# Shared-expert down projections dealt over the token table of a routed expert layer, with the fillers, PSUM pools and first rows around the routing rearranged

## The chip, the cores and the metric

The kernel runs on one core of a Trainium2 chip. The metric is the device time of one execution in microseconds, given as the median of three runs. Engines are named as in the profile: PE is TensorE (PEld its weight loads), DVE is VectorE, ACT is ScalarE, POOL is GpSimd, SP issues most of the DMAs.

## What is computed

The input is x, 16 batches of 128 rows with 512 features, and a context of 16 times 128 rows with 128 features. The reference is one attention block and one mixture of experts, each added to x:

```python
x = x + _L0_xattn_ref(_layernorm(x, axis=-1), ctx_512, ctx_512)
x = x + _L0_ffn_ref(_layernorm(x, axis=-1), gate_weight, e_bias, w1, w2, w3, shared_w1, shared_w2, shared_w3)
...
    tidx, tw = _gate(x, gate_weight, e_bias)      # sigmoid, 4 of 8 groups, then 8 of 32 experts
    g = jnp.einsum('td,eid->tei', x, w1)
    u = jnp.einsum('td,eid->tei', x, w3)
    a = jax.nn.silu(g) * u
    routed = jnp.einsum('tei,edi,te->td', a, w2, comb)
    sh = jax.nn.silu(x @ shared_w1.T) * (x @ shared_w3.T) @ shared_w2.T
    out = routed + sh
```

There are 2048 tokens, each with 8 of 32 experts; an expert has 256 hidden features. The shared expert takes every token.

## The kernel before

A batch of 128 rows is one tile of 128 partitions. The order of the instructions on TensorE, VectorE, ScalarE and GpSimd is the order in which the program writes them (a manual schedule); each engine takes its own in that order, and a framework puts in the semaphores. The DMAs of SP stand in its queue in program order too. The work has four stages.

Attention (`attention_small`, to about 124 us) loops over 32 items, two halves of the heads for each of 16 batches. An item n issues its scores (line 430), the values of item n - 1 (446), the transposed queries of a later batch (`queries`, 417, with a copy on VectorE in 421), a few matmuls that only keep TensorE busy (`keep_warm`), and the output of item n - 2 (`added`). Lists named head and tail hang other steps onto an item, among them the layer norm's statistics (`layernorm_stats`), its inverse deviation (`first_rstd`, 11 small VectorE instructions) and the normalized rows (`rows_of`, 394). Before the loop stand the statistics of batches 0 and 1, then one `first_rstd` for both, then both rows, then the keys and values; `queries(0)` comes ahead of item 0, and `queries(b)` in item 2b - 2.

Routing (`route` in `experts`, about 133 to 165 us) is one long chain on VectorE: sigmoid scores, group sums, a comparison of groups (gt, eq, gm), masked scores (ms), a max8 and a match-replace for each of 16 batches, and the selection sel (1278). Then TensorE counts the tokens of each expert (1286, 1294) and ranks them (1316 to 1360).

To fill TensorE meanwhile, the up projections of the shared expert are a generator of single matmuls (`shared_up`, 253): 8 pieces of 8 matmuls of 512 columns, each piece a gate g (4 matmuls) and an up u (4), for 512 tokens and half of the hidden features. After g a silu on ScalarE is due (261), after u a product on VectorE (264, tile sa); both are put in lists and issued where the program says. The first piece uses two banks of a tile gu in the pool of the scores. The other 7 take banks from the pool ps_gu, two banks, opened when that pool has closed. `up_matmuls(n)` issues the next n of their 56 matmuls: 22 ahead of the routing's chain, 4 and 6 after the ranks, then 2 in each slot of the token table. In the chain, the product of the first piece stands behind gs, product0 (the second piece) behind the sum gt and ahead of gm, product1 (the third piece) behind the ninth max8.

The token table (165 to 214 us) lists which token stands at which place. Its loop has 16 slots, one per batch. A slot builds one-hot tiles hr (1076) and 6 of 8 hq (1085) on VectorE, the 2 other hq on GpSimd, ht (1083) on ScalarE, and adds 8 small matmuls to tok (1091). Each of hr, hq and ht has two buffers. Products and silus that wait are called between hq and the matmuls of a slot; a product waits one slot more in a list named held. In slots 4, 9 and 14 one shared down is issued (`shared_down`: four 512-column pieces on TensorE, 1420, two f32 matmuls), whose sum with x (1430) goes the way of the products, followed by a DMA of x to out. After the loop `finish_tokens` (1102, 1103) makes token, and the 13 other downs follow, each with its sum and its DMA.

The expert stage (236 us to the end) gathers 138 slices of 128 rows by indirect DMAs of GpSimd (1498), five ahead, transposes them (1512, copy 1514), runs the up matmuls (1534) and downs (1588), and scatters the weighted rows onto out by accumulating DMAs (1560). Weights of three experts are held; their first loads are issued from 163 us on.

At the end a flag is read. If an expert has more tokens than its capacity, or the attention's keys are too long, a general path behind a branch is run: the general attention, the experts again, and tiles of left-over tokens. With this input it isn't taken.

Of the kernel before, what the change touches and what calls it, by code (L numbers as in the profile page):

```python
# [43 lines left out]
def tile_xattn_moe(  # L44
# [24 lines left out]
    NTILES = (NT * P * TOPK + E * (P - 1)) // P  # L69
    LT = -(-NTILES // NW)  # L70
    NQT = LT * NW

# [199 lines left out]
    def attention_small():  # L272


        with ExitStack() as ph:
# [128 lines left out]
            for b in range(2):  # L404
                layernorm_stats(b, mv1)
            first_rstd(0, 2)
            for b in range(2):
                rows_of(b)
# [116 lines left out]

            for b, n in ((4, 1), (5, 1), (6, 2), (7, 2)):
                at_tail(n, layernorm_stats, b, mv1)
            for b in (2, 3):
                at_head(0, layernorm_stats, b, mv1)
            at_tail(0, first_rstd, 2, 2)  # L530
            at_tail(0, rows_of, 2)
# [41 lines left out]
            for n in range(N):  # L573
                for f, a in head.get(n, ()):
                    f(*a)

                scores(*items[n])
                if n > 0:
                    values(*items[n - 1])
                if n in parts:  # L580
                    gate_parts(parts[n])
                if n % 2 == 0 and n // 2 + 1 < B:
                    queries(n // 2 + 1)
                keep_warm(FILL.get(n, 0))
                if n in sums:
                    gate_sums(sums[n])
                if n > 1:
                    added(*items[n - 2])
                if n in turned:
                    gate_turn(turned[n], ps_tr)  # L590
                for f, a in tail.get(n, ()):
                    f(*a)
# [3 lines left out]
            ps_sc.tile([P, 2, G, P], F32, tag="sc", name="sc")  # L596
# [166 lines left out]
    def tile_work(ctx, token, owner, load_e):  # L763

        flat = out.rearrange("b s d -> (b s) d")
        wp = ctx.enter_context(tc.tile_pool(name="wp", bufs=1))

        wup = [wp.tile([P, 2, ND, I], F32, name=f"wup{r}") for r in range(NW)]  # L770
        wdn = [wp.tile([P, NI, D], F32, name=f"wdn{r}") for r in range(NW)]


        NG_BUF = 6
        xgs = [wp.tile([P, D + E], F32, name=f"xg{r}") for r in range(NG_BUF)]
        for t in xgs:
            nc.gpsimd.memset(t, 0.0)

        ps_gu = ctx.enter_context(tc.tile_pool(name="ps_gu", bufs=2, space=PSUM))
        ps_y = ctx.enter_context(tc.tile_pool(name="ps_y", bufs=2, space=PSUM))  # L780
        tp = ctx.enter_context(tc.tile_pool(name="tp", bufs=3))
        ps_a = ctx.enter_context(tc.tile_pool(name="ps_a", bufs=1, space=PSUM))
        ps_x = ctx.enter_context(tc.tile_pool(name="ps_x", bufs=2, space=PSUM))
        xg, xT, gus, al, aTs, last = {}, {}, {}, {}, {}, []

        def load_weights(q):
            r = q % NW
            with tc.issue_after(last[0]) if last else nullcontext():
                _, (e, new_e) = nc.values_load_multi_w_load_instructions(
                    load_e[0:1, :, q],  # L790
                    engines=[mybir.EngineType.SP],
                    min_val=0,
                    max_val=E - 1,
                    skip_runtime_bounds_check_because="experts' numbers and flags",
                    bass_reorder=False,
                )
            for dst, src in ((wup[r][:, 0], w1), (wup[r][:, 1], w3), (wdn[r], w2)):
                dma = nc.sync.dma_start(
                    dst,
                    src[bass.ds(e, 1)].rearrange("o p a b -> (o p) a b"),  # L800
                    **({} if q < NW else dict(cond=new_e, bounds_check="skip_entire_dma")),
                )
            last[:] = [dma.ins]

        def gather(q):
            t = xgs[q % NG_BUF]
            nc.gpsimd.indirect_dma_start(
                out=t,
                out_offset=None,
                in_=rows[:, :],  # L810
                in_offset=bass.IndirectOffsetOnAxis(ap=token[:, q : q + 1], axis=0),
                bounds_check=NT * P - 1,
                oob_is_err=False,
            )
            xg[q] = t

        def turn(q):
            tr = ps_x.tile([P, ND, P], F32, tag="trx", name="trx")
            for k in range(ND):
                nc.tensor.transpose(tr[:, k, :], xg[q][:, ts(k, P)], ident)  # L820
            t = tp.tile([P, ND, P], F32, tag="xT", name="xT")
            nc.scalar.copy(t, tr)
            xT[q] = t

        def up(q, ds):
            if 0 in ds:
                gus[q] = ps_gu.tile([P, 2, I], F32, tag="gu", name="gu")
            for d in ds:
                nc.tensor.matmul(
                    gus[q],  # L830
                    lhsT=xT[q][:, d, :],
                    rhs=wup[q % NW][:, :, d, :],
                    start=(d == 0),
                    stop=(d == ND - 1),
                )

        def gated(q):
            gu = gus.pop(q)
            del xT[q]
            sl = tp.tile([P, I], F32, tag="sl", name="sl")  # L840
            nc.scalar.activation(sl, gu[:, 0, :], AF.Silu)
            a = tp.tile([P, I], F32, tag="a", name="a")
            nc.vector.tensor_tensor(a, sl, gu[:, 1, :], ALU.mult)
            own = tp.tile([P, E], F32, tag="own", name="own")
            wt = tp.tile([P, 1], F32, tag="wt", name="wt")
            nc.vector.scalar_tensor_tensor(
                own,
                expert,
                owner[:, q : q + 1],
                xg.pop(q)[:, D:],  # L850
                ALU.is_equal,
                ALU.mult,
                accum_out=wt,
            )
            al[q] = a, wt

        def gated_turn(q):
            at = ps_a.tile([P, NI, P], F32, tag="at", name="at")
            for i in range(NI):
                nc.tensor.transpose(at[:, i, :], al[q][0][:, ts(i, P)], ident)  # L860
            aT = tp.tile([P, NI, P], F32, tag="aT", name="aT")
            nc.vector.tensor_copy(aT, at)
            aTs[q] = aT

        def down(q):
            aT, wt = aTs.pop(q), al.pop(q)[1]
            y = ps_y.tile([P, D], F32, tag="y", name="y")
            for i in range(NI):
                nc.tensor.matmul(
                    y,  # L870
                    lhsT=aT[:, i, :],
                    rhs=wdn[q % NW][:, i, :],
                    start=(i == 0),
                    stop=(i == NI - 1),
                )
            yw = tp.tile([P, D], F32, tag="yw", name="yw")
            nc.scalar.activation(yw, y, AF.Copy, scale=wt)
            nc.gpsimd.indirect_dma_start(
                out=flat,
                out_offset=bass.IndirectOffsetOnAxis(ap=token[:, q : q + 1], axis=0),  # L880
                in_=yw,
                in_offset=None,
                compute_op=ALU.add,
                bounds_check=NT * P - 1,
                oob_is_err=False,
            )

        def run(first, end):
            last.clear()
            for n in range(first - 4, end + 1):  # L890
                if first <= n + 4 < end:
                    gather(n + 4)
                if first <= n < end:
                    up(n, range(ND - 1))
                if first <= n - 1:
                    gated_turn(n - 1)
                if first <= n + 1 < end:
                    turn(n + 1)
                if first <= n < end:
                    up(n, [ND - 1])  # L900
                    gated(n)
                if first <= n - 1:
                    down(n - 1)
                if first <= n + 2 < end:
                    load_weights(n + 2)

        return run

    def rest():

        with ExitStack() as ctx:
            keep = ctx.enter_context(tc.tile_pool(name="keep", bufs=1))
            token = keep.tile([P, NQT], I32, name="token")
            owner = keep.tile([P, NQT], F32, name="owner")
            load_e = keep.tile([P, 2, NQT], I32, name="load_e")
            rounds = keep.tile([1, 1], I32, name="rounds")
# [816 lines left out]
```

## Time and profile before

| what | us |
|---|---|
| median of 3 runs | 1034.4 (1032.83 to 1034.75) |
| the profiled execution, its own time | 1034.52 |
| its span in the trace | 1032.7 |
| PE busy | 999.4 |
| POOL busy | 508.5 |
| ACT busy | 325.9 |
| DVE busy | 255.2 |
| VectorE's wait for a filler ahead of product0 | 3.58 |
| TensorE's waits for VectorE's one-hots, two | 0.96 and 2.27 |
| start of the first expert transpose | 236.13 |

Times within the trace count from the span's start. A row of the timeline has the start, the time to the end, the engine, the line, the operation, the tiles written and read, how many instructions were merged into it, and in brackets how long the engine was idle before it and what ended the idle time. An f32 matmul of the program appears as two in the trace. A row of the stage table has a stretch, its length, then the busy time of PE, PEld, DVE, ACT and POOL with their instruction counts, the granted TensorE clock (1.00 is full), the DMA share and GB/s.

### The profile page before, as it was taken

How to read it: one execution, taken by the hardware profiler on the slowest of the kernel's cores; microseconds unless marked ns; L12 is line 12 of the kernel's file. 1: busy time of each engine (PE TensorE's matmuls, PEld its weight loads, DVE VectorE, ACT ScalarE, POOL GpSimd, SP SyncE). 2: the span in 40 equal slices, each digit the busy share in tenths (PEclk: the TensorE clock that was granted, in tenths of full speed). 3: DMA queues.
4: the chain of work that ended last, by engine and by line, in shares of the span. 5: the costliest groups of instructions: out<-in, count | busy, mean ns of one | idle time of the engine just before them, and what ended most of it. 6: DMA issues, size and time to landing. Idle time of an engine off the chain costs nothing.

```text
span 1032.7 us, 12455 instructions
## 1 busy us (share of the span) xinstructions
PE 999.4 (97%) x4176; PEld 575.9 (56%) x4176; DVE 255.2 (25%) x902; ACT 325.9 (32%) x517; POOL 508.5 (49%) x658
## 2 busy tenths in 40 slices
PE   8999998999999999999999999999999999999993
PEld 5344444447666556676766666666644444444462
DVE  7887668951011000111111101101110010010100
ACT  5676612402222222232323232323222322322220
POOL 4588534732445445454545454545453445454342
PEclk9999999999999999999999999999999999999997
DMA  9011105053666757775757676767674766665541
GB/s 307 3 42 52 52 22 193 22 177 87 169 141 152 156 131 164 163 163 125 184 130 179 140 166 144 163 146 164 144 194 116 172 157 150 152 151 136 118 58 26
DMA packets 59865, 137.07 MB, mean 133 GB/s; under 512 B 12168, under 2 KB 16392, under 8 KB 59792
## 3 DMA queue, kind: packets, MB, share of 16 engines
q0 software_dynamic: 32032, 69.25, 35.5%
q1 hardware_dynamic: 27680, 66.81, 19.3%
q8 instruction: 35, 0.57, 0.2%
q14 instruction: 38, 0.31, 0.1%
q10 hardware_dynamic: 80, 0.13, 0.0%
HBM read 96.71 MB, written 46.73 MB: 139 GB/s over the span
## 4 chain that ended last, share of the span: by engine, by line
PE 64%; issue 5%; DMA 4%; POOL 3%; POOLq 0%; ACT 0%
PE gu L1534 40%; PE y L1588 19%; PE trx L1512 5%; DMA out_dram<-yw,token 4%; POOL out_dram L1560 2%; POOL xg L1498 1%; ACT xnT L1514 0%; POOLq L1560 0%; POOLq L1498 0%; POOLq L1659 0%
## 5 line engine op out<-in xcount | busy, mean ns | idle before, releaser
L1534 PE MATMUL gu<-xnT,wup 128*128 128x256 f32 (+8 forms) x1664 | 501.9, 450 | 2.4 <-ACT xnT L1514 2.4
L1534 PEld LDWEIGHTS gu<-xnT,wup 128*128 128x128 f32 x1664 | 313.1, 190 | 200.0 <-issue 134.1
L1560 POOL DMA_INDIRECT out_dram<-yw,token x150 | 235.7, 1571 | 368.0 <-ACT yw L1597 265.0
L1588 PE MATMUL y<-wdn,sa 128*128 128x512 f32 (+2 forms) x672 | 260.1, 594 | 0.0
L1545 DVE TENSOR_TENSOR sa<-sl,gu 128x256 f32<-128x256 f32 (+8 forms) x104 | 52.9, 508 | 699.0 <-PE gu L1534 681.8
L1498 POOL DMA_INDIRECT xg<-rows,token x138 | 145.3, 1053 | 61.1 <-issue 33.2
L1597 ACT ACTIVATE yw<-y,wt 128x512 f32<-128x512 f32 x138 | 94.8, 687 | 179.1 <-PE y L1588 153.9
L1588 PEld LDWEIGHTS y<-wdn,sa 128*128 128x128 f32 (+2 forms) x672 | 92.4, 171 | 72.7 <-issue 71.0
L1514 ACT COPY xnT<-trx 128x512 f32<-128x512 f32 (+3 forms) x150 | 81.3, 551 | 158.6 <-PE trx L1512 149.4
L1543 ACT ACTIVATE sl<-gu 128x256 f32<-128x256 f32 (+8 forms) x104 | 47.1, 453 | 247.7 <-PE gu L1534 243.0
L1512 PEld LDWEIGHTS trx<-ident,xg 128*128 128x128 f32 x552 | 69.0, 141 | 37.1 <-issue 26.2
L1512 PE MATMUL trx<-ident,xg 128*128 128x128 f32 x552 | 82.7, 273 | 0.0
L440 ACT ACTIVATE p<-sc 128x1024 f32<-128x1024 f32 x64 | 62.1, 1021 | 29.5 <-PE sc L430 29.5
L253 PE MATMUL gu<-xnT,sup 128*128 128x512 f32 x128 | 61.2, 617 | 3.9 <-ACT ssl L261 2.2
L1085 POOL TENSOR_SCALAR hq<-slice_q,sq 128x138 f16<-128x138 f16 x32 | 31.8, 1005 | 35.2 <-DVE sq L1386 23.0
L430 PE MATMUL sc<-qT,kz 32*128 32x512 f32 x256 | 41.8, 639 | 0.0
L253 PEld LDWEIGHTS gu<-xnT,sup 128*128 128x128 f32 x128 | 23.3, 195 | 28.4 <-issue 22.5
L446 PE MATMUL oT<-p,va 128*32 128x512 f32 x256 | 34.1, 605 | 1.1 <-DVE oTs L455 1.1
L475 POOL TENSOR_TENSOR x<-x,at 128x256 f32<-128x256 f32 x32 | 23.4, 734 | 22.8 <-DVE at L468 22.7
L1519 DVE SCALAR_TENSOR_TENSOR own<-expert,owner,xg 128x32 f32<-128x32 f32 x138 | 31.6, 246 | 0.0
L1420 PE MATMUL y<-sdn,sa 128*128 128x512 f32 x64 | 29.5, 615 | 0.0
L1083 ACT ACTIVATE ht<-hr,token 128x1024 f16<-128x1024 f16 x16 | 18.4, 1148 | 25.4 <-DVE hr L1076 22.6
(178 smaller groups left out, 468.2 us busy)
## 6 DMA issues: line engine op xcount, KB each, us to landing
wup<-in_w_dram SPq DMA_DIRECT2D x64, 512.0 KB
wdn<-in_w_dram SPq DMA_DIRECT2D x32, 512.0 KB
rows<-xn SPq DMA_DIRECT2D x16, 256.0 KB
out_dram<-x SPq DMA_DIRECT2D x16, 256.0 KB
x<-in_x_dram SPq DMA_DIRECT2D x15, 256.0 KB
out_dram<-yw,token POOLq DMA_INDIRECT x150
xg<-rows,token POOLq DMA_INDIRECT x138
cTs<-in_cT_dram SPq DMA_DIRECT2D x4, 256.0 KB
```

What stands on the lines that cost most here:

```text
L253: nc.tensor.matmul(acc, lhsT=sup[:, w, d, ts(i, P)], rhs=xnT[k][:, d, :], start=(d == 0), stop=(d == ND - 1),)
L430: nc.tensor.matmul(scs[j // 2][:, j % 2], lhsT=kzs[b // 4 % 2][rows, b % 4, i, :], rhs=qTs[b][rows], start=True, stop=True, tile_position= ...
L440: nc.scalar.activation(p, sc, AF.Exp, scale=1.0 / HD**0.5)
L1498: nc.gpsimd.indirect_dma_start(out=t, out_offset=None, in_=rows[:, :], in_offset=bass.IndirectOffsetOnAxis(ap=token[:, j : j + 1], axis=0) ...
L1512: nc.tensor.transpose(tr[:, d, :], t[:, ts(d, P)], ident)
L1514: nc.scalar.copy(xnT[n % NTB][:, :, col : col + b - a], tr[:, :, a:b])
L1534: nc.tensor.matmul(acc[:, 0:m], lhsT=wup[k % NW][:, w, d, ts(i, P)], rhs=xnT[n % NTB][:, d, 0:m], start=(d == 0), stop=(d == ND - 1),)
L1543: nc.scalar.activation(banks[2][:, 0:m], acc[:, 0:m], AF.Silu)
L1545: nc.vector.tensor_tensor(acts[n % NTB][:, i, 0:m], banks[2][:, 0:m], acc[:, 0:m], ALU.mult)
L1560: ins = nc.gpsimd.indirect_dma_start(out=flat, out_offset=bass.IndirectOffsetOnAxis(ap=token2[:, k - 1 : k] if a else token[0:b, j : j + 1 ...
L1588: nc.tensor.matmul(y[c0:c1, :], lhsT=acts[n % NTB][:, i, col : col + c1 - c0], rhs=wdn[pieces[n][0] % NW][:, i, :], start=(i == 0), stop=( ...
L1597: nc.scalar.activation(yws[j], y, AF.Copy, scale=wt[:, j : j + 1])
```

## The change

It has four parts.

1. Ahead of the attention's loop stand the statistics, `first_rstd` and rows of batch 0 alone, then the statistics of batch 1. One `first_rstd` for batches 1 to 3 stands at the tail of item 0 with the row of batch 1; the row of batch 2 goes to the tail of item 1. The queries of batch 1 go from item 0 to item 1, ahead of `queries(2)` in item 2.
2. Around the routing: 20 fillers instead of 22 ahead of the chain, 4 and 9 instead of 4 and 6 after the ranks; product0 behind ms instead of ahead of gm. An unused tile that turned the pool of the scores by one is dropped, and the pools ps_gu and ps_y are opened in the other order. In the built program the first piece stays in banks 0 and 1 and the later pieces move from banks 0 and 1 to 2 and 3, the downs the other way.
3. The shared downs: one in each odd slot from 1 to 11, two in each of slots 12 to 14, one in slot 15, and 3 after the table. In slots 13 to 15 the products and sums no longer wait the further slot.
4. The general path behind the branch is another one: it reads the rows and logits back, and runs every expert over every token, weighted by zero where the main path did the work. The number of left-over tiles and its loops are gone.

The main path's instructions are the same in number but for one wait, and the order on ScalarE, GpSimd and SP is the same; on TensorE and VectorE the order differs as said.

```diff
             fixed_values(0, nc.vector)
-            for b in range(2):
-                layernorm_stats(b, mv1)
-            first_rstd(0, 2)
-            for b in range(2):
-                rows_of(b)
+            layernorm_stats(0, mv1)
+            first_rstd(0, 1)
+            rows_of(0)
+            layernorm_stats(1, mv1)
...
+            for b in (2, 3):
+                at_head(0, layernorm_stats, b, mv1)
+            at_tail(0, first_rstd, 1, 3)
+            at_tail(0, rows_of, 1)
+            at_tail(1, rows_of, 2)
             for b, n in ((4, 1), (5, 1), (6, 2), (7, 2)):
                 at_tail(n, layernorm_stats, b, mv1)
-            for b in (2, 3):
-                at_head(0, layernorm_stats, b, mv1)
-            at_tail(0, first_rstd, 2, 2)
-            at_tail(0, rows_of, 2)
...
-                if n % 2 == 0 and n // 2 + 1 < B:
+                if (n == 1 or n % 2 == 0 and n > 0) and n // 2 + 1 < B:
                     queries(n // 2 + 1)
...
-            ps_sc.tile([P, 2, G, P], F32, tag="sc", name="sc")
             gu = ps_sc.tile([P, 2, G, P], F32, tag="sc", name="gu")
...
+        ps_y = ctx.enter_context(tc.tile_pool(name="ps_y", bufs=2, space=PSUM))
         ps_gu = ctx.enter_context(tc.tile_pool(name="ps_gu", bufs=2, space=PSUM))
-        ps_y = ctx.enter_context(tc.tile_pool(name="ps_y", bufs=2, space=PSUM))
...
-            up_matmuls(22)
+            up_matmuls(20)
...
             nc.vector.tensor_tensor(gt, gt, eq, ALU.add)
-            product0()
             gm = new([P, NQ], "gm")
...
             nc.vector.tensor_scalar(ms, ms, 0.0, None, ALU.add)
+            product0()
...
-            up_matmuls(6)
+            up_matmuls(9)
...
             held = list(products)
+            if b > NT - NTB:
+                meanwhile += held
+                held.clear()
             later.clear()
...
             up_matmuls(2)
-            if b % 5 == 4:
+
+            for _ in range(b % 2 if b < NT - NTB else 2 if b < NT - 1 else 1):
                 shared_down(next(downs))
...
     with tc.If(left > 0, preferred_fallthrough_block=False):
-        flag = nc.values_load(
...
-        with tc.If(flag > 0):
-            attention_general()
-            experts(pieces, ExitStack(), [], [])
         rest()
```

## The prediction

> **What bounds the kernel now.** I read the page first, then TensorE's waits, then the timelines of TensorE and VectorE around the routing, then a table by stage. The page:
>
> ```profile
> PE 999.4 (97%) x4176; PEld 575.9 (56%) x4176; DVE 255.2 (25%) x902; ACT 325.9 (32%) x517; POOL 508.5 (49%) x658
> PE 64%; issue 5%; DMA 4%; POOL 3%; POOLq 0%; ACT 0%
> ```
>
> TensorE is busy for 97% and carries the chain that ended last. The view of TensorE's waits, cut to the time after 240 us, has one row of 1.7 us (on the copy xnT of line 1514): the expert stage has next to no slack, so it starts later or earlier as a block, with its tail of scatter DMAs. The change touches nothing in it. So I ask only when its first transpose (236.13 us) starts. TensorE before it:
>
> ```profile
> 137.65 19.15 PE L253 MATMUL gu<-xnT,sup 128*128 128x512 f32 x44 [1.70 <-DVE sa L264]
> 157.23 0.55 PE L1286 MATMUL count<-ones,sel 128*32 128x1 f16 x16 [0.43 <-DVE sel L1278]
> ...
> 160.68 5.42 PE L253 MATMUL gu<-xnT,sup 128*128 128x512 f32 x12
> 168.32 5.40 PE L253 MATMUL gu<-xnT,sup 128*128 128x512 f32 x8 [2.23 <-ACT ssl L261]
> 173.56 0.66 PE L1091 MATMUL tok<-hq,ht 128*128 128x138 f16 x8
> 174.05 1.93 PE L253 MATMUL gu<-xnT,sup 128*128 128x512 f32 x4
> ...
> 206.40 0.67 PE L1091 MATMUL tok<-hq,ht 128*128 128x138 f16 x8 [0.96 <-DVE hq L1085]
> 209.33 0.67 PE L1091 MATMUL tok<-hq,ht 128*128 128x138 f16 x8 [2.27 <-DVE hq L1085]
> 209.84 2.96 PE L1420 MATMUL y<-sdn,sa 128*128 128x512 f32 x4
> 212.60 1.12 PE L1091 MATMUL tok<-hq,ht 128*128 128x138 f16 x8
> 213.52 22.77 PE L1420 MATMUL y<-sdn,sa 128*128 128x512 f32 x52
> 236.13 1.04 PE L1512 MATMUL trx<-ident,xg 128*128 128x128 f32 x8
> ```
>
> A row counts each f32 matmul of the program twice. From 204.8 to 213.5 TensorE waits for VectorE's one-hot tiles (hq), while 13 shared downs stand idle until 213.52. The gaps are followed by slow rows: 8 pieces took 5.40 us, against 19.15/44 = 0.435 us a piece elsewhere. The stage table, whose third number from the end is the granted clock, says why:
>
> ```profile
> 168.35:173.56 5.21, 5.21 (x9) 2.10 (x10) 2.08 (x8) 1.15 (x1) 1.69 (x2) 0.67 1.00 403
> 204.80:213.52 8.72, 5.49 (x38) 3.28 (x36) 6.56 (x22) 3.44 (x3) 4.25 (x5) 0.83 0.01 2
> ```
>
> VectorE in the routing:
>
> ```profile
> 144.89 0.69 DVE L264 TENSOR_TENSOR sa<-ssl,gu 128x512 f32<-128x512 f32 x1 [3.58 <-PE gu L253]
> 151.76 0.69 DVE L264 TENSOR_TENSOR sa<-ssl,gu 128x512 f32<-128x512 f32 x1
> 156.49 0.69 DVE L1278 TENSOR_TENSOR sel<-rp,ms 128x512 f16<-128x512 f32 x1
> 213.76 0.30 DVE L1102 TENSOR_SCALAR empty<-tok 128x138 f32<-128x138 f32 x1 [2.40 <-PE tok L1091]
> ```
>
> **What the skill says.** The Trainium skill, "TensorE: Matmul & The Clock Gate", section "What's actually happening": the clock falls to half after a mostly idle window of 3413 ns; windows run free. The trace agrees: 0.50 granted from about 169.6 to 173 us and from about 210.4 to 213.8, after windows with 2.2 and 2.3 us of idle; the 1.70 us of idle before 137.65 left it at 1.00. "DMA: Bandwidth & Descriptors", section "Anatomy of one DMA — SWDGE (gpsimd) path": about 2.0 us plus bytes/436e3. A gather of 128 rows of 2176 bytes is then an estimated 2.6 us behind its issue of 1.0 to 1.3. Agrees: the gather issued at 214.71 had its 0.28 MB moved by 218.5 in the DMA view.
>
> **Part 1, rows of batch 0 alone.** The chain from statistics 0 to row 0 no longer waits for statistics 1: it begins at 4.82 instead of 6.25, -1.43 us. Behind row 0 on VectorE now stands statistics 1 (0.85), which fits under the four transposes (the copy qT starts 8.70, was 10.12). Scores 0, exp 0, scores 1 and values 0 all come 1.43 earlier (values 0 at 13.75, was 15.17). But the transposes of batch 1 now follow values 0: copy oTs at 14.93, copy qT at 15.53, and scores 0.80 behind it: item 2 at 16.33, where it was 16.16. It then no longer waits for ScalarE (0.27 saved), so values 1 starts at 17.40 against 17.51. Row 1 waits for x of batches 1 to 3 (landed before 9.2, since the later-queued cn landed at 9.18); it is ready at 14.15, needed at 14.74. Sum **-0.1 us**; bounds -1.4 (all kept) and +0.7 (row 1 late).
>
> **Part 2, product moved and 20 for 22 fillers.** Moving product0 behind ms lets VectorE run on instead of idling 3.58 us, so it reaches product1 at about 149.0. But product1 needs the 16th filler matmul: 137.65 + 32 x 0.4288 is 151.4, and it already started at 151.76 as TensorE ended. So it waits there 2.7 us and sel stays at 156.49: nothing gained. The banks swap places, yet in the built order the first filler of the second piece still waits for the first product (the 1.70 us above), so that stays too; bounds -1.7 and 0, taken 0. With two fillers fewer TensorE stops at 155.1 and idles 2.2 us before the counts.
>
> After the counts (160.68 in both) 4 + 9 fillers stand in place of 4 + 6. The 8 before the next wait take 8 x 0.858 + 0.27, to 167.8; ScalarE's silu then gives 168.6 (it gave 168.32). The idle there falls from 2.23 to 0.8, so this window should not halve the clock. Net **+0.3 us** at the start of that matmul, and the same 28 fillers are left in both.
>
> **Part 3, the spread downs.** Work from there: 28 fillers (4 at 0.87, 2 lone ones at 0.86, 11 pairs at 1.77 as between 174.05 and 175.82) 24.7; 16 table groups at 0.49, 7.85; 16 downs at 22.61/13 = 1.74, 27.8; sum 60.4. Before took 236.13 - 168.32 = 67.8, so 7.4 was lost: half clock 1.97 and about 1.6, waits 0.38 + 0.96 + 2.27. If these go, the expert stage starts at 168.6 + 60.4 = 229.0: **-7.1 us**, part 2's 0.3 within it.
>
> Does VectorE keep up? A slot costs it 1.14 (hr) + 1.15 (hq) = 2.29, against TensorE's 2.26 without a down, 4.0 with one, 3.97 with two and no fillers. It gets 10 more adds of 0.6 ahead of the table, 6.0, but its 3.39 us wait at 173.82 shrinks by 1.5. In the built order an add stands behind the one-hots of a later slot than its down, so TensorE has a table group and new downs while VectorE adds. In slots 13 to 15 VectorE needs 0.3 + 1.2 + 2.3 = 3.8 per slot from the end of a pair of downs, TensorE 0.49 + 3.48 = 3.97: 0.2 to slack. GpSimd's two hq take about 2.1 of the 4 us between table groups. The SP queue has the same 16 writes of out, now from slot 3 on, behind the loads of expert weights that ended by 174.
>
> The cover: 13 downs (22 us) hid the gathers; now 4 do, 7.0 us. Table end 222.0, token and gather issue 0.95 + 0.3, landing 3.6 more: about 227, the second 1.6 later at 228.5; needed at 229.0 and 229.5. Cost 0, up to +2 (plus 1.7 of half clock) if landings spread as between 220 and 227.7, where seven gathers took 1.9 us each beside the writes.
>
> **Part 4, the dense path** stands behind a branch that is not taken: no instruction of it runs. Taken 0, bounds -0.3 and +0.3.
>
> Sum: -0.1 - 7.1 = -7.2 us. The profiled execution took 1034.52 (span 1032.7), 0.12 above the median 1034.4: **1027.3**.
>
> **Rivals.** (a) The idle before the counts halves the clock: its window holds 1.3 us of idle, then 32 tiny matmuls; half clock over the rank matmuls and first fillers costs about 1.5: 1028.8. For: two such windows above; against: 1.70 us of idle did not. (b) Gathers uncovered: +2 to +3.5: 1030.3. (c) The slots fall partly into step, losing 0.45 each of 16: 1034.4, no change. (d) Slower: VectorE's adds wait in its queue for y ahead of the next one-hots, and TensorE waits for those. Full lockstep is 0.49 + 3.48 + 0.3 + 0.6 + 2.3 = 7.2 a slot against 4.0, over 9 slots +29; half of it ends at 1034.5 - 7.2 + 14 = 1041. It decides against the change from 7.2/9 = 0.8 us a slot on. Against it speaks the slot of lead. (e) The wait on the banks or on product1 does not bind as I read it: 1.5 to 3 better, 1025.
>
> **Chances.** Forecast 0.58 (own range 1025.5 to 1029), a 0.17, b 0.08, c 0.05, d 0.05, e 0.07. About 0.2% (2 us) is what a measurement can tell from no change: faster 0.90, same 0.05, slower 0.05. The range 1024.0 to 1031.5 takes in forecast, a, b and e.
>
> **What would show it.** VectorE idle about 2.7 us ahead of the product between the max8 steps; TensorE idle 2.2 before count and under 1 before the u of the fifth piece; clock 1.00 at 168 to 214; no wait for hq over 0.5; first expert transpose near 229, no wait for xg over 1. Wrong if rows tok wait for hq in each slot, or trx waits for a gather.

## The result, and the profile after

| | before | after |
|---|---|---|
| median | 1033.62 us (4 runs) | 1024.76 us (4 runs, 1022.55 to 1025.06) |
| ratio, 95% interval | | 0.9909 [0.9891, 0.9927], so -9.4 us [-11.3, -7.5] |
| profiled execution, its own time | 1034.52 | 1022.55 |
| its span | 1032.7 | 1020.8 |
| first expert transpose | 236.13 | 230.21 |
| from there to the start of the last scatter's issue | 781.59 | 782.24 |
| from there to the end of the span | 15.02 | 8.33 |

The change is faster: 9.4 us are gained where 7.2 were forecast, and the median is 2.5 us under the forecast of 1027.3. The last three rows already say that the forecast's own account is wrong: the expert stage starts 5.9 us earlier and not 7.1, it gets 0.65 us longer, and 6.7 us are won at the very end, where the forecast put nothing (-5.92 + 0.65 - 6.69 = -11.96, the difference of the two spans).

The page of the kernel after, the two lines that answer to those of before:

```profile
PE 996.8 (98%) x4176; PEld 574.3 (56%) x4176; DVE 254.3 (25%) x902; ACT 326.2 (32%) x517; POOL 513.1 (50%) x658
PE 77%; POOL 9%; issue 7%; DVE 4%; DMA 2%; ACT 1%; POOLq 0%; DVEq 0%; ACTq 0%
```

TensorE's work is the same. Its timeline around the routing (start, time to the end, in brackets the idle time ahead):

```profile
137.39 17.43 PE L250 MATMUL gu<-xnT,sup 128*128 128x512 f32 x40 [1.72 <-DVE sa L261]
156.96 0.55 PE L1135 MATMUL count<-ones,sel 128*32 128x1 f16 x16 [2.14 <-DVE sel L1127]
...
159.93 1.75 PE L1167 MATMUL rank<-sel,ones 128*128 128x352 f16 x11
161.99 7.13 PE L250 MATMUL gu<-xnT,sup 128*128 128x512 f32 x16
169.87 4.56 PE L250 MATMUL gu<-xnT,sup 128*128 128x512 f32 x10 [0.75 <-ACT ssl L258]
...
223.29 7.08 PE L1269 MATMUL y<-sdn,sa 128*128 128x512 f32 x16
230.21 0.60 PE L1365 MATMUL trx<-ident,xg 128*128 128x128 f32 x4
231.29 0.66 PE L1365 MATMUL trx<-ident,xg 128*128 128x128 f32 x4 [0.49 <-DMA xg<-rows,token]
```

The waits for one-hot tiles are gone: from 174 to 230 TensorE has no wait. The bank wait (1.72) and the 2.14 us ahead of the counts are there as forecast. The fillers behind the ranks start at 161.99, not at 160.7. The table by stage shows why (its third number from the end is the granted clock):

```profile
157.92:161.33 3.41, 3.41 (x17) 1.54 (x14) 2.02 (x10) 0.00 (x0) 0.00 (x0) 0.50 0.00 0
161.33:164.70 3.37, 3.37 (x17) 1.74 (x16) 2.49 (x13) 0.59 (x1) 0.00 (x0) 1.00 0.00 0
```

Half clock lay over the rank matmuls: rival (a). On VectorE the third piece's product (product1) waits as forecast, and sel starts at 156.22:

```profile
151.50 0.69 DVE L261 TENSOR_TENSOR sa<-ssl,gu 128x512 f32<-128x512 f32 x1 [2.67 <-PE gu L250]
```

Last, the end of GpSimd's stream: the issue of the last scatter in the timeline, then rows of the view by source line, for the branch and for the kernel's end (number of instructions, shortest, median and longest in ns, start of the first and last). Before:

```profile
1017.71 1.57 POOL L1560 DMA_INDIRECT out_dram<-yw,token  x1 [0.30 <-issue]
L1665 POOLq EVENT_SEMAPHORE  x6: 17/30/43, 1018.0 to 1021.6; - x6
L1665 POOLq COMPARE_BRANCH  x2: 41/42/43, 1017.9 to 1023.4; - x2
L1665 POOLq INC_SWDGE_SEM  x1: 1612/1612/1612, 1021.7 to 1021.7; - x1
L1729 POOLq DRAIN  x3: 46/107/5982, 1025.9 to 1032.5; - x3
```

After:

```profile
1012.45 1.57 POOL L1413 DMA_INDIRECT out_dram<-yw,token  x1 [0.30 <-issue]
L1518 POOLq COMPARE_BRANCH  x2: 41/42/43, 1012.6 to 1012.9; - x2
L1518 POOLq EVENT_SEMAPHORE  x2: 17/17/17, 1012.7 to 1012.8; - x2
L1573 POOLq DRAIN  x3: 46/113/6562, 1013.4 to 1020.5; - x3
```

In the kernel before GpSimd enters the short side of the branch, the one that skips the general path, at 1017.9, 0.2 us behind the start of its last scatter. It waits there for its eight DMA lanes (the eight semaphores in which its DMAs report in turn) until 1021.7, runs an instruction of 1.6 us that counts the lanes' semaphores up (INC_SWDGE_SEM), and jumps to the kernel's end at 1023.4. There its long Drain instruction starts at 1025.9, and the other engines wait for that Drain at the last barrier. In the kernel after it jumps at 1012.9 and the Drain starts at 1013.4, beside the scatter that is still on its way. The built program says where the waits come from: on the short side, each engine brings every semaphore to the value that the general path would have left. The old general path issues gathers and scatters from GpSimd, on all eight lanes; the dense path issues none.

### The profile page after: what moved, and what is told of

Read it like the earlier page. It is cut to its first block, busy times and chain, and to the rows that moved or that the text cites. A ratio compares the mean times of both kernels' runs of the same rounds, so it can differ in the third digit from the quotient of the medians.

```text
span 1020.8 us, 12451 instructions
## 1 busy us (share of the span) xinstructions
PE 996.8 (98%) x4176; PEld 574.3 (56%) x4176; DVE 254.3 (25%) x902; ACT 326.2 (32%) x517; POOL 513.1 (50%) x658
## 4 chain that ended last, share of the span: by engine, by line
PE 77%; POOL 9%; issue 7%; DVE 4%; DMA 2%; ACT 1%; POOLq 0%; DVEq 0%; ACTq 0%
PE gu L1387 44%; PE y L1441 21%; PE trx L1365 6%; PE gu L250 3%; POOL hq L935 2%; POOL out_dram L1413 2%; POOL xn L214 2%; DMA out_dram<-yw,token 1%; POOL x L471 1%; PE sc L426 1%; DVE st L88 1%; POOL kz L347 1%; PE oT L442 1%; DMA xg<-rows,token 0%; DVE oTs L451 0%
## 5 line engine op out<-in xcount | busy, mean ns | idle before, releaser
L935 POOL TENSOR_SCALAR hq<-slice_q,sq 128x138 f16<-128x138 f16 x32 | 35.2, 1113 | 40.8 <-DVE sq L1235 24.6
```

The lines of the kernel that those rows point to most:

```text
L935: engine(k).tensor_scalar(hq[:, k, :], tile_q, sq[:, b, k : k + 1], None, ALU.is_equal)
```

## The experiments

Theory T, formed from these two traces: of the gain, 6.7 us at the end are part 4's. The rival is the prediction on record: part 4 is worth 0, and part 3's 7.1 us carry the change. Times are compared as ratios with runs of the kernel before taken beside each experiment on the same chip (three sets of runs, medians 1032.9, 1032.8 and 1034.5).

**Part 4 alone.** The kernel before with the dense path in `rest`, and the old `tile_work` and the two calls behind the branch gone.

```diff
     with tc.If(left > 0, preferred_fallthrough_block=False):
-        flag = nc.values_load(
...
-        with tc.If(flag > 0):
-            attention_general()
-            experts(pieces, ExitStack(), [], [])
         rest()
```

> The kernel before with part 4 alone (the dense path behind the branch; nothing else). As the prediction has it, part 4 costs nothing: 1033.6, and the expert stage as well as the end as before. Theory T, formed from the two traces: in the kernel before GpSimd waits, on the side of the branch that is taken, until the last scatters have landed, and only then begins the Drain of about 6 us that closes the kernel; the new path behind the branch issues no DMA from GpSimd, so that this wait is not there and the Drain runs beside the last scatter. T expects the stretch from the start of the last scatter's issue to the end of the span to fall from 15.0 to about 8.4 us, the first expert transpose to stay at 236.1, and 1027.0 in all.

Measured 1027.75 us, ratio 0.9949 [0.9937, 0.9962], -5.3 us. In its profile the last stretch is 8.33 us, as in the kernel after. The end, in the view by source line:

```profile
L1516 POOLq COMPARE_BRANCH  x2: 41/42/43, 1016.2 to 1016.4; - x2
L1571 POOLq DRAIN  x3: 46/113/6563, 1016.9 to 1024.0; - x3
```

The transposes start at 234.39, not 236.1, for a reason outside this part: this execution had one stretch of half clock, the profiled one of before two. Part 4 is not free of effect; the prediction's zero falls. The trace's 6.69 us lie just outside the interval of the times, 3.9 to 6.5. With five runs, half clock that falls in some executions and not in others can make that difference, but this is not shown.

**Part 3 alone.**

```diff
             held = list(products)
+            if b > NT - NTB:
+                meanwhile += held
+                held.clear()
...
-            if b % 5 == 4:
+            for _ in range(b % 2 if b < NT - NTB else 2 if b < NT - 1 else 1):
                 shared_down(next(downs))
```

> The kernel before with part 3 alone (the spread downs, 22 and 6 fillers as before). As the prediction has it: first expert transpose at 228.7 (236.1 less 7.4), no wait for one-hots over 0.5 us, clock 1.00 from 168 to 214, and 1033.6 - 7.4 = 1026.2. Rival: the gathers are not covered, the transposes wait for them, and half clock stays somewhere: transpose at 230 to 232, 1028 to 1030. Either way the end stays as before: 15 us from the start of the last scatter's issue to the end of the span.

Measured 1029.16 us, ratio 0.9963 [0.9948, 0.9977], -3.8 us: half of what was forecast for it. No wait for one-hots is left. But the profile shows half clock behind TensorE's 2.21 us of idle time ahead of the matmul that needs the silu, the transposes of the second slice wait 0.77 us for its gather, and the first start at 230.34. The rival of this run holds. TensorE's timeline:

```profile
168.31 5.40 PE L253 MATMUL gu<-xnT,sup 128*128 128x512 f32 x8 [2.21 <-ACT ssl L261]
231.70 0.66 PE L1516 MATMUL trx<-ident,xg 128*128 128x128 f32 x4 [0.77 <-DMA xg<-rows,token]
```

**Eight gathers behind the branch.** The kernel after; `idx` is an index tile, and none of these gathers is run.

```diff
             comb = keep.tile([P, NT, E], F32, name="comb")
...
+            got = keep.tile([P, D + E], F32, name="got")
+            for _ in range(8):
+                nc.gpsimd.indirect_dma_start(
+                    out=got,
...
```

> The kernel after, with eight gathers issued by GpSimd added in the path behind the branch, which is not run with this input; all instructions that are run ahead of the branch are the same. If part 4 costs nothing (the prediction), 1024.8 as the kernel after. Theory T: the waits of GpSimd for its eight DMA lanes come back on the side of the branch that is run, the Drain starts only after them, and the stretch from the start of the last scatter's issue to the end is 15 us again: 1024.8 + 6.6 = 1031.4, with the first expert transpose at 230.2 as in the kernel after.

Measured 1028.64 us, ratio to before 0.9951 [0.9937, 0.9965] where the kernel after had 0.9909; the last stretch is 12.73 us instead of 8.33. What is built ahead of the branch is the same, instruction for instruction. Instructions that never run cost 4.4 us, through the waits that they put on the short side. The rows of the branch and the end in the view of source lines, of this run:

```profile
L1530 POOLq COMPARE_BRANCH  x2: 41/42/43, 1011.8 to 1017.1; - x2
L1530 POOLq INC_SWDGE_SEM  x1: 1612/1612/1612, 1015.4 to 1015.4; - x1
L1585 POOLq DRAIN  x3: 46/107/5982, 1017.5 to 1024.1; - x3
```

The theory's 15 us were too many by 2.3: the Drain follows the jump 0.4 us later here and 2.5 us later in the kernel before. So a second cost remained, which the run with memsets takes alone.

**22, 4 and 7 fillers.** The kernel after with TensorE's idle time ahead of the counts filled again.

```diff
-            up_matmuls(20)
+            up_matmuls(22)
...
-            up_matmuls(9)
+            up_matmuls(7)
```

> The kernel after with 22 fillers ahead of the chain and 4 and 7 behind the ranks (20, 4 and 9 in the kernel after): the two fillers go back into TensorE's idle time ahead of the counts. Theory H (the half clock over the rank matmuls comes from that idle time, rival a of the prediction): idle ahead of the counts 0.4 instead of 2.1 us, clock 1.00 from 157 to 162, fillers behind the ranks start at 160.4 instead of 162.0, and the expert stage 1.3 to 1.6 us earlier: 1023.3. Rival: the idle time moves to the next wait (the u of the fifth piece waits for its silu, as in the kernel before with 2.2 us), halves the clock there, and nothing is gained: 1024.8.

Measured 1022.96 us, ratio to before 0.9894 [0.9879, 0.9908]; the kernel after had 0.9909 and, below, 0.9900. The time can't tell them apart. In the profile theory H is right at its place (idle 0.43 us ahead of the counts, fillers at 160.41, full clock) and so is its rival one step on: the wait for the silu is 2.21 us again and half clock follows it. TensorE's timeline of this run:

```profile
156.96 0.55 PE L1135 MATMUL count<-ones,sel 128*32 128x1 f16 x16 [0.43 <-DVE sel L1127]
160.41 5.42 PE L250 MATMUL gu<-xnT,sup 128*128 128x512 f32 x12
168.03 6.25 PE L250 MATMUL gu<-xnT,sup 128*128 128x512 f32 x10 [2.21 <-ACT ssl L258]
```

**Memsets behind the branch.** The kernel after, with no DMA of GpSimd behind the branch but 190 more instructions of its own there.

```diff
+            pad = keep.tile([P, 1], F32, name="pad")
+            for _ in range(190):
+                nc.gpsimd.memset(pad, 0.0)
```

> The kernel after with 190 small memsets for GpSimd added in the path behind the branch, which is not run: as many GpSimd instructions behind the branch as in the kernel before, but no DMA of GpSimd. In the kernel before 2.5 us pass between the end of GpSimd's branch and its Drain, in the kernel after 0.5. Theory J: that jump is longer where more of GpSimd's own instructions lie behind the branch; 2.5 us here too, the stretch from the last scatter's issue to the end 10.4 instead of 8.3, 1026.9. Rival: the jump goes with the waits for the DMA lanes, not with the length; 8.3 us and 1024.8 as the kernel after.

Measured 1026.75 us, ratio to before 0.9937 [0.9923, 0.9951] where the kernel after had 0.9909, and the last stretch is 10.79 us, 2.46 more. The Drain starts 3.5 us behind the jump, with no wait between them, as the same view of this run shows:

```profile
L1521 POOLq COMPARE_BRANCH  x2: 41/42/43, 1011.4 to 1011.6; - x2
L1576 POOLq DRAIN  x3: 46/107/5988, 1015.1 to 1021.7; - x3
```

Theory J's rival falls: the jump gets longer with no DMA behind the branch. J itself holds only in part, for the jump takes 3.5 us and not 2.5, and it does not grow with the number of instructions. In the built programs GpSimd jumps over some 90 of its instructions in the kernel after, 110 with the gathers, 280 with the memsets and 2100 in the kernel before; the jumps take 0.46, 0.46, 3.49 and 2.55 us. That is a step between 110 and 280 instructions, not a slope.

A step fits what the Trainium skill, "Runtime: NRT & Kernel Launch", section "Instruction fetch mechanics", says of a branch that is taken: if the target lies outside the fetched window, its page must be loaded before the engine goes on. The DMA view agrees where it is clear of other engines: cut to the jump of the kernel before (1023.36 to 1025.89) it has a single packet, of an instruction queue; cut to that of the gathers' run (1017.08 to 1017.53) it has none. Why the load takes 2.5 us in one kernel and 3.5 in another is not known.

So part 4's 6.7 us are 5.2 of waiting and counting up (5.64 and 0.46 us from the start of the last issue to the jump), 2.1 of a longer jump, less 0.6 because the Drain takes 6.56 beside a scatter and 5.98 otherwise.

**Part 2 alone.** The kernel before with 20, 4 and 9 fillers, product0 behind ms and the pools in the other order.

```diff
-            up_matmuls(22)
+            up_matmuls(20)
...
-            product0()
             gm = new([P, NQ], "gm")
...
             nc.vector.tensor_scalar(ms, ms, 0.0, None, ALU.add)
+            product0()
...
-            up_matmuls(6)
+            up_matmuls(9)
```

> The kernel before with part 2 alone (20 fillers ahead of the chain, 4 and 9 behind the ranks, product0 behind ms, the pools in the other order). The prediction: sel starts where it did (156.5), TensorE idles 2.2 us ahead of the counts at full clock behind it, the idle time ahead of the next silu falls from 2.2 to 0.8 us with no half clock behind it: 0.3 us lost and 2.0 of half clock won against the profiled execution of before. Rival a: the half clock moves from the silu's gap to the counts; the rank matmuls end 1.3 us later, nothing is won, and the time is that of the kernel before, 1032.9, within 1 us.

Measured 1035.8 us, ratio 1.0020 [1.0012, 1.0029], so 2.1 us slower, which neither the prediction nor the rival had. In the profile the wait for the silu does fall to 0.75, but the time is given back to the one-hot tiles, and half clock of two stretches begins within the second wait. TensorE's timeline of this run:

```profile
205.48 0.67 PE L1090 MATMUL tok<-hq,ht 128*128 128x138 f16 x8 [1.67 <-DVE hq L1084]
208.41 1.10 PE L1090 MATMUL tok<-hq,ht 128*128 128x138 f16 x8 [2.27 <-DVE hq L1084]
```

Without the spread downs the end of the table is VectorE's, so TensorE gains nothing by reaching it earlier. The 2.1 us are not in this profile: it is the shortest of the 13 runs (1034.36), and its span is that of the profiled run of before. The clock on record shows them as more half clock: the granted clock is 0.9894 in the mean of the 13 runs and 0.9914 in that of the 18 runs of before beside them, and 0.0020 of 1033 us is 2.1. Which gap it follows in those runs is not seen.

**Part 1 alone.**

```diff
-            for b in range(2):
-                layernorm_stats(b, mv1)
-            first_rstd(0, 2)
-            for b in range(2):
-                rows_of(b)
+            layernorm_stats(0, mv1)
+            first_rstd(0, 1)
+            rows_of(0)
+            layernorm_stats(1, mv1)
...
```

> The kernel before with part 1 alone (rows of batch 0 first). The prediction: 0.1 us faster, bounds -1.4 and +0.7; by the trace of the kernel after, the values of item 1 come at 17.15 instead of 17.51 and the routing 0.3 us earlier. So 1032.5 to 1032.7 against 1032.8, which the time cannot tell from no change; the trace should show values 1 at 17.15 and the first filler behind the bank wait at 137.4. Rival (all of the 1.4 us is kept): values 1 at 16.1 and 1031.4.

Measured 1033.06 us, ratio 0.9993 [0.9985, 1.0001], -0.7 us: not to be told from nothing. In this profile the values of item 1 start at 17.82 and the first filler behind the bank wait at 138.07. The forecast's 0.1 us can't be told here: profiles of the same instructions ahead of the routing differ by 0.6 us in when that filler starts (137.39, 137.46, 137.73 and 137.98 in the four of the kernel after and of those that differ from it only behind the branch). Neither trace shows the larger bound, -1.4 (values at 16.1).

**All but part 2.** Parts 1, 3 and 4 as above, part 2's lines as before.

> The kernel before with parts 1, 3 and 4, that is, the kernel after without part 2. If the parts add up as they did alone (part 4 -5.1, part 3 -3.7, part 1 -0.2), 1023.8, and part 2 is worth +1 in the kernel after. If part 2 is worth its 1.4 us less of waiting for the silu once the spread downs keep it (in the kernel before it was given back to the one-hot tiles), 1026. The trace should show 0.4 us of idle ahead of the counts and 2.2 us ahead of the silu, and half clock behind the latter in some executions.

Measured 1022.88 us, ratio 0.9894 [0.9879, 0.9909], under both of the expected times, and, in the same set of runs, **the kernel after once more**:

> The kernel after itself once more, for the spread of its executions: 1024.8, with single runs from 1022.5 to 1027, as the half clock behind the 2.1 us of idle ahead of the counts falls in some executions and not in others. If the profile has no half clock there, the fillers behind the ranks start at 160.4 and not at 162.0, and the first expert transpose stands at about 228.7 instead of 230.2.

Measured 1023.13 us, ratio 0.9900 [0.9884, 0.9916]. With and without part 2 the times are the same within their intervals; these are too wide to say whether the 2.1 us that part 2 costs alone are there. In this second profile of the kernel after, the half clock behind the counts lasts twice as long, and the transposes start at 232.15. Its table by stage:

```profile
155.83:159.24 3.41, 1.93 (x37) 1.27 (x37) 2.82 (x12) 0.00 (x0) 0.00 (x0) 1.00 0.00 0
159.24:162.65 3.41, 3.41 (x18) 2.23 (x18) 1.84 (x9) 0.00 (x0) 0.00 (x0) 0.50 0.00 0
162.65:166.06 3.41, 3.41 (x5) 1.35 (x4) 3.24 (x23) 0.58 (x1) 0.00 (x0) 0.50 0.03 6
```

**A better version, in two steps.** First the kernel of the 22, 4 and 7 fillers with the silu issued where its input ends, ahead of the first slot's copy ht on ScalarE; then one down moved from slot 1 to behind the table.

```diff
             up_matmuls(7)
+            for silu in later:
+                silu()
+            later.clear()
```

> The kernel after with 22, 4 and 7 fillers (as in the run e4_fillers_22_7) and the silu of the fourth piece issued right behind the fillers that follow the ranks, ahead of the first table slot's copy on ScalarE. In e4 TensorE waited 2.2 us for that silu, which stood behind the copy ht of slot 0. Theory: the wait falls to 0.7 us (the silu's own time), no half clock behind it, and the expert stage starts 1.5 us earlier, 3.2 where e4 had half clock there: 1020.5 against 1023.0. Rival: VectorE or the gathers become late instead (a wait for hq, or for xg over 1.6 us), and the gain is given back: 1023.0.

Measured 1021.01 us, ratio 0.9876 [0.9860, 0.9891]. The wait for the silu is 0.75 us, no half clock follows it, and the transposes start at 227.29. The second slice's gather is now late by 1.14 us, and half clock follows that, as this run's table by stage shows:

```profile
227.31:230.72 3.41, 1.59 (x11) 1.09 (x10) 1.38 (x7) 1.17 (x2) 2.80 (x3) 1.00 1.02 362
230.72:234.13 3.41, 3.41 (x11) 2.68 (x10) 0.00 (x0) 0.13 (x1) 2.03 (x3) 0.50 0.95 345
```

```diff
-            for _ in range(b % 2 if b < NT - NTB else 2 if b < NT - 1 else 1):
+            for _ in range(b % 2 if 1 < b < NT - NTB else 0 if b < 2 else 2 if b < NT - 1 else 1):
```

> As c1_silu_early, and the shared down of slot 1 is put behind the table, so that five downs instead of four stand between the end of the table and the first expert transpose (8.7 instead of 7.0 us). Theory: the gathers are then covered, the transposes' wait for xg of 0.5 to 1.6 us goes, and it is 0.5 to 1.6 us faster than c1: 1019.5. Rival: the waits for xg are set by transfers that crowd one another, they stay, and it is c1's time.

Measured 1018.87 us (1018.62 to 1018.93), ratio 0.9858 [0.9844, 0.9873]. The two measurements of the kernel after had 0.9909 and 0.9900, so this is 4 to 5 us faster than it. It is 2.1 us under the first step, more than the theory's 1.6, which left out the half clock behind the wait. The wait for the gather is gone, all eight transposes stand in one row, and no half clock is left between the first microseconds and the last scatter. TensorE's timeline of this run:

```profile
226.93 1.04 PE L1368 MATMUL trx<-ident,xg 128*128 128x128 f32 x8
228.70 1.99 PE L1390 MATMUL gu<-xnT,wup 128*128 128x256 f32 x8 [0.73 <-ACT xnT L1370]
```

## Why the prediction came out as it did

The table takes the profiled executions apart. The second column counts the stretches of 3.41 us at half clock ahead of the expert stage, by the clock records ("behind" is one within that stage). The third is the time from the first filler behind the bank wait to the first expert transpose, less 1.71 us, half of 3.41, for each stretch ahead of it: the waits and the work alone. The fourth is the expert stage to the start of the last scatter's issue, the fifth the rest.

| kernel | half-clock stretches | fillers to transpose, at full clock | expert stage | end |
|---|---|---|---|---|
| before | 2 | 95.1 | 781.59 | 15.02 |
| part 1 | 1 | 95.0 | 781.59 | 15.11 |
| part 2 | 2 | 95.2 | 781.59 | 14.66 |
| part 3 | 1 | 91.0 | 782.52 | 14.80 |
| part 4 | 1 | 95.0 | 781.58 | 8.33 |
| parts 1, 3, 4 | 1 | 91.0 | 782.67 | 8.33 |
| after | 1 | 91.1 | 782.24 | 8.33 |
| after, again | 2 | 91.0 | 782.65 | 8.33 |
| after, gathers behind the branch | 0 | 91.2 | 782.42 | 12.73 |
| after, memsets behind the branch | 0 | 91.2 | 782.47 | 10.79 |
| after, 22, 4 and 7 | 1, and 1 behind | 91.0 | 785.06 | 8.33 |
| silu early | 0, and 1 behind | 89.7 | 784.58 | 8.33 |
| silu early, cover | 0 | 89.7 | 781.59 | 8.33 |

- **Part 1, -0.1 us**: within what can't be told. The values of item 1 started at 17.15 where 17.40 was forecast, but a profile's start shifts by 0.6 us anyway. The path was right: the scores of item 2 wait for the copy qT of batch 1 (0.92 us).
- **Part 2, "nothing gained" on VectorE, +0.3 on TensorE**: sel, the wait at product1 (2.67 for a forecast 2.7), the bank wait and the idle time ahead of the counts came as worked out. The sentence "so this window should not halve the clock" was right too: behind the silu's gap of 0.75 us the clock was full in all seven profiles that have it. What failed is that this was counted as won, for the gap of 2.1 us ahead of the counts took its place. That is rival (a), which was given 0.17: half clock followed that gap in 2 of 5 profiles, the silu's gap of 2.2 us in 4 of 6.
- **Part 3, -7.1 us**: two terms. The waits, 0.38 + 0.96 + 2.27 = 3.6 us, measured 4.0 (95.1 to 91.1 us); that VectorE would keep up was right (no row of the table waits for a one-hot tile, which also rules out rivals (c) and (d)), and 229.0 for the first transpose is what executions without half clock show (228.70 with the memsets, 229.21 with the gathers). The other term, 3.6 us of half clock, is the one that was mis-sized. It was read off one execution, with two stretches (3.4 us by the clock records; the forecast's 1.97 for one of them has the end of a row, 0.27, in it), and taken as won. The single times of before lie in groups some 1.6 us apart, with the profiled one in the third: of the 47 runs beside the experiments 2 are at 1031, 20 at 1032.4 to 1033.1, 22 at 1034.0 to 1034.8 and 3 at 1036. If the groups are 0 to 3 stretches, they average 1.6. The nine runs of the kernel after fall into 1022.6 to 1023.1 (four, the profile with one stretch among them), 1024.8 to 1025.1 (four, the profile with two) and 1026.4: 1.7. On average no half clock was won; the same idle time stands at another place. The granted clock on record for each run fits: its mean falls from 0.9945 over 0.9923 and 0.9907 to 0.9890 in the four groups of before, and one stretch is worth half of 3.41 us in 1033, 0.0017. Where the half clock lies in a run without a trace is not seen.
- **The gathers, "cost 0, up to +2"**: the expert stage is 0.65 to 1.1 us longer in the profiles with four covering downs, 3.0 and 3.5 in the two where half clock follows the wait, and no longer at all with five. The second slice landed 0.5 to 1.6 us late, where the forecast had 1.0 to spare: part of rival (b), which was given 0.08. The step that failed is "the second 1.6 later": at 80 packets a gather, the second's packets end 2.4 us behind the first's in the kernel after (230.65 and 228.28), and they did so 2.5 us behind in the kernel before (220.91 and 218.41), from which the forecast could have taken it. (Its 1.9 us a gather is the mean from the first issue at 214.71 to 227.7, not from 220.)
- **"so it starts later or earlier as a block, with its tail of scatter DMAs"**: right for the stage (781.59 us in five kernels, to 0.01), wrong for the tail. **Part 4, "Taken 0, bounds -0.3 and +0.3"** is the step that failed outright, since "no instruction of it runs" does not make it free: the end takes 8.33 us in every kernel with the dense path alone and 14.7 to 15.1 in every one without it. The page of before held the hint: in the last of its 40 slices (25.8 us) TensorE was busy for three tenths, and the span went on for 15 us behind the start of the last scatter's issue. No row of busy time and no row of the chain of waits names what filled them, since waiting, branching and Drain instructions are not counted there.

In sum: -4.0 (waits) - 6.7 (end) + 0.9 (gathers, the mean of six profiles) + 0.2 (half clock, 1.6 to 1.7 stretches) = -9.6 us; measured were -9.4 [-11.3, -7.5] and, in the second measurement, -10.3 [-12.0, -8.7]. The forecast's -7.2 was near by luck, through two errors of opposite sign: 3.6 us of half clock that was not won, and 6.7 us at the end that were not seen. Rival (e) named the time that came, 1025, with a cause that did not: the waits on the banks (1.72 us) and at product1 (2.67) both stand. And of the forecast's own signs all came but the first transpose near 229; none of them looks at the end.

## What to carry to other kernels

Read the end of a trace instruction by instruction, with the ones that count as no work: a path that is never run can set what the side that skips it waits for, and how long its jump takes. Count half clock not as lost time of one profile but as a chance for each gap of TensorE; moving a gap does not remove it, while issuing the late producer earlier does (here one silu, 1.3 us of wait and the half clock with it). When filler work is spread forward, keep as much of it behind the last index as the gathers need.

## What the runs showed of the hardware

- **What halves the clock.** The Trainium skill, "TensorE: Matmul & The Clock Gate", section "What's actually happening", has a free-running window of 3413 ns; the clock records agree, since every change in a trace lies a whole number of 3.41 us from the others. The page speaks of an idle window; here a window that is idle for about 2.0 us of its 3.41 is enough. Set on that grid, windows with up to 1.40 us of busy time were followed by half clock (1.31 in before, ahead of 169.63; 1.40 in part 4 alone, ahead of 208.99), and windows with 1.53 and 1.57 us of 512-column f32 matmuls were not (part 4 alone; gathers behind the branch). So the same gap of 2.2 us halves the clock or not by where the grid falls. Two windows don't fit one limit: 1.59 us, mostly transposes (silu early), and 1.93 us, mostly counts (after, again), were followed by half clock. That small matmuls count for less would explain these two, but not a window of 1.57 us, mostly 128-column matmuls (part 4 alone, 7.61 to 11.02), behind which the clock stayed full. What is counted was not tried by itself and stays open.
- **GpSimd's last Drain** takes 5.98 us with its scatters landed and 6.56 us with the last one on its way, the same to 0.01 us in each of the 13 profiles, and the barrier waits for it. INC_SWDGE_SEM takes 1.61 us.
